# Graph attention on one Trainium2 core: Q by edge made two batches ahead and kept in SBUF, E in two PSUM banks a batch ahead

## The chip, the core and the metric

The kernel runs on one core of a Trainium2 chip. The metric is device time in microseconds (us), from one launch. The engines are named as the profile names them: PE is TensorE (PEld its weight loads), DVE is VectorE, ACT is ScalarE, POOL is GpSimd, SP is SyncE. PSUM has eight banks, and all eight are in use before and after.

## What is computed

The reference is one layer of graph attention with a residual and a layer norm, over 6250 nodes and 206250 edges (sorted by `dst`), 128 features, 8 heads of 16:

```python
Qh, Kh, Vh = h @ WQ, h @ WK, h @ WV            # N x 8 x 16
Eh = edge_attr @ WE                            # E x 8 x 16
score = einsum('ehd,ehd,ehd->eh', Kh[src], Qh[dst], Eh) / sqrt(16)
score = exp(clip(score, -5, 5))
wV = segment_sum(Vh[src] * score[:, :, None], dst, N)
Z  = segment_sum(score, dst, N)
out = layernorm(x + wV / (Z + 1e-6))
```

## The kernel before

The edges are cut into 1612 tiles of 128 edges, and the tiles into 406 batches, of four tiles each but for the last few. At the start a table of K and V rows is made for all nodes (`table`) and written to HBM as `kv`. Each tile then gathers its 128 rows of `kv` by `src` with one indirect DMA that POOL issues (`gather`, L315), four for a batch. The first `XB` = 12 batches gather rows of `x` and make K and V on the core (`project`); the others gather from `kv`.

Q by edge is not gathered. `dst` is sorted, so an edge tile needs few neighbouring nodes. `q_rows` makes Q for a block of 128 nodes, as three bf16 parts, and stores it to HBM (`qs`). `load_q` loads a window of 42 nodes for each 8 tiles, and a matmul of this window with a one-hot of the edges' nodes (`onehotT`) spreads Q over the 512 edges of a batch, with features on partitions. E for the same edges is a matmul of `we_sb` with the edge attributes. Both lie as features x edges.

One round of the main loop serves several batches. In round b the steps below are issued, in this order:

- `turn`(b-1): four transposes bring Q x E of the batch before to edges x features (tile `pps`).
- `stage_a`(b): Q's matmul (tile `qps`), ScalarE's copy of it to SBUF (`qT`), and E's matmul (tile `eps`).
- `finish`, once in some 16 rounds: block sums of two windows of nodes (tile `finps`), then the layer norm's steps, which `fill` strews between VectorE's other work.
- `stage_b`(b-2) on VectorE: `kq` = gathered K rows x `pps`, the sum per head, and the clip (`sc`).
- `messages`(b-3) on VectorE: V rows x weights (`msg`).
- `stage_0`(b+2) on VectorE: the two one-hots (`onehot`, `onehotT`) of a batch two rounds ahead (`AHEAD` = 2).
- `pairs`(b) on VectorE: `eq` = `qT` x `eps`.
- `weigh`(b-2) on ScalarE: the exponentials, twice.
- `stage_c`(b-3): four matmuls add the messages into the window's sum (tile `agg`), and ScalarE copies a finished sum.
- `q_rows`, once in some 8 rounds: Q of the next 128 nodes (tile `qrows`).

From round `XB` on, instructions stand on each engine in the order in which the code issues them (`manual_schedule`); before that a scheduler may move them. Each engine works its list in order. Waits come from tiles: a tile's buffer is used again only when its last reader is done.

PSUM's eight banks are `psE` (1: `eps`), `psQ` (1: `qps`), `psP` (2: `pps`), `psT` (1: `qrows`, `finps`, the transposes of `project`, the count), `psA` (2: `agg`) and `psX` (1: constants and exponentials). The table's blocks and the products of `project` (`kvps`) go in turn through the banks of `psE`, `psP` and `psQ` (`pair_bank`).

Gathers are paced. The pool of gathered rows has `GB` = 15 buffers, so the gather of batch b waits for `messages`(b-15). From batch `LOCK` = 16 on, the first of a batch's four gathers waits also for Q's matmul of batch b - lag(b), where lag falls by one each 4 batches from 12 to `STEP` = 1:

```python
def lag(b):
    return max(STEP, 12 - (b - LOCK) // 4)
...
if i == 0 and b >= LOCK:
    made = expanded[b - lag(b)]
```

SyncE issues the other loads and stores: edge attributes in 512 KB chunks, the nodes of edges spread over partitions (`relb`), Q's windows, rows of `x`, and the output.

Of the kernel before, what the change touches and what calls it, by code (L numbers as in the profile page):

```python
# [24 lines left out]
MW = D + H  # L25
B = 4
CH = 8
GB = 15
XB = 12
LOCK = XB + 4  # L30
STEP = 1
TAIL = 8
HEAD = 132
NG = (NT + G - 1) // G
AHEAD = 2
EB = 6
SLAG = 2
WT = 8
RC = 16
# [41 lines left out]
def edge_attention(ctx: ExitStack, tc: tile.TileContext, x, xT, srcT, dstT, dstB, dst0, bnd, lo, eaT,  # L81
# [30 lines left out]
    with ExitStack() as fast:  # L112
# [78 lines left out]
        def count_inside():  # L191

            W = 4 * 2 * D
            for a in range(0, NT, W):
                e = min(NT, a + W)
                cl = wp.tile([P, W], F32, name="cl", tag="kvst", bufs=2)[:, :e - a]
                count(P, cl, rel[:, a:e], P - 1)
            nc.vector.tensor_reduce(cn[:, :1], cn, axis=AX.X, op=ALU.add)
            pc = psT.tile([1, 1], F32, name="pc", tag="oT")
            nc.tensor.matmul(pc, cn[:, :1], ones, start=True, stop=True)  # L200
            nc.vector.tensor_copy(cnt_i, pc)

# [1 line left out]
        ep = fast.enter_context(tc.tile_pool(name="edges", bufs=EB))  # L204
        wp = fast.enter_context(tc.tile_pool(name="work", bufs=3))
        sp = fast.enter_context(tc.tile_pool(name="sums", bufs=7))
        psE = fast.enter_context(tc.tile_pool(name="psE", bufs=1, space=bass.MemoryType.PSUM))
        psQ = fast.enter_context(tc.tile_pool(name="psQ", bufs=1, space=bass.MemoryType.PSUM))
        psP = fast.enter_context(tc.tile_pool(name="psP", bufs=2, space=bass.MemoryType.PSUM))
        psT = fast.enter_context(tc.tile_pool(name="psT", bufs=1, space=bass.MemoryType.PSUM))  # L210
        psA = fast.enter_context(tc.tile_pool(name="psA", bufs=2, space=bass.MemoryType.PSUM))
        psX = fast.enter_context(tc.tile_pool(name="psX", bufs=1, space=bass.MemoryType.PSUM))

# [3 lines left out]

        def pair_bank(i, name, shape):

            pool, tag = ((psE, "eps"), (psP, "pps"), (psQ, "qps"), (psP, "pps"))[i % 4]  # L220
            return pool.tile(shape, F32, name=name, tag=tag)


# [31 lines left out]

        def q_rows(q):
            n = min(P, N - q * P)
            ps = psT.tile([P, D], F32, name="qrows", tag="oT")
            nc.tensor.matmul(ps[:n], xT_sb[:, LEFT + q * P:LEFT + q * P + n], wq_sb, start=True, stop=True)
            st = wp.tile([P, QP, D], BF16, name="qst", bufs=1)  # L260
            r1 = wp.tile([P, D], F32, name="qr1", bufs=1)
            nc.scalar.copy(st[:n, 0, :], ps[:n])  # L262
            nc.vector.tensor_tensor(r1[:n], ps[:n], st[:n, 0, :], op=ALU.subtract)  # L263
            nc.scalar.copy(st[:n, 1, :], r1[:n])
            nc.vector.tensor_tensor(st[:n, 2, :], r1[:n], st[:n, 1, :], op=ALU.subtract)
            nc.sync.dma_start(qs[q * P * QP:(q * P + n) * QP].rearrange("(p s) f -> p s f", s=QP), st[:n])
            built.append(q)
# [20 lines left out]
        chunks, aggs, sums, pair_sums, st8, expanded = {}, {}, {}, {}, {}, {}  # L288

        def load_chunk(c):  # L290
            if c in chunks or c * CH >= NT:
# [33 lines left out]

        def project(g, n):

            pt = psT.tile([P, B, P], F32, name="xtps", tag="oT")
            for i in range(n):
                nc.tensor.transpose(pt[:, i, :], g[:, i, :D], ident)  # L330
            xgT = wp.tile([P, B, P], F32, name="xgT", tag="kq", bufs=2)
            nc.scalar.copy(xgT[:, :n], pt[:, :n])
            for i in range(0, n, 2):
                k = min(2, n - i)
                pk = pair_bank(i // 2, "kvps", [P, 2, 2 * D])
                for j in range(k):
                    nc.tensor.matmul(pk[:, j, :], xgT[:, i + j, :], wkv_sb, start=True, stop=True)  # L337
                nc.scalar.copy(g[:, i:i + k, :], pk[:, :k, :])  # L338

        def stage_0(b):  # L340
            t0, n = batches[b][0], len(batches[b])
            oh = wp.tile([P, B, P], F32, name="onehot", bufs=AHEAD + 5)
            nc.vector.tensor_tensor(oh[:, :n], iota_p[:, None, :].to_broadcast([P, n, P]),  # L343
                                    rel[:, t0:t0 + n, None].to_broadcast([P, n, P]), op=ALU.is_equal)
            ohT = wp.tile([QROWS, B * P], BF16, name="onehotT", bufs=AHEAD + 2)
            e0 = t0 % RC * P
            nc.vector.tensor_scalar(ohT[:, :n * P], rels[t0 // RC][:, e0:e0 + n * P], node[:QROWS], None,  # L347
                                    op0=ALU.is_equal)
            st8[b] = oh, ohT

        def stage_a(b, g):
            t0, n = batches[b][0], len(batches[b])
            if b < XB:
                project(g, n)
            oh, ohT = st8.pop(b)
            pq = psQ.tile([P, B * P], F32, name="qps")
            expanded[b] = nc.tensor.matmul(pq[:, :n * P], loaded[t0 // WT], ohT[:, :n * P], start=True, stop=True)  # L357
            qT = wp.tile([P, B * P], F32, name="qT", bufs=2)
            nc.scalar.copy(qT[:, :n * P], pq[:, :n * P])  # L359
            pe = psE.tile([P, B * P], F32, name="eps")  # L360
            nc.tensor.matmul(pe[:, :n * P], we_sb, ea_tiles(t0, n), start=True, stop=True)  # L361
            st8[b] = [n, g, oh, pe, qT]

        def pairs(b):

            n, g, oh, pe, qT = st8[b]
            eq = wp.tile([P, B * P], F32, name="eq", bufs=2)
            nc.vector.tensor_tensor(eq[:, :n * P], qT[:, :n * P], pe[:, :n * P], op=ALU.mult)  # L368
            st8[b] = [n, g, oh, eq]
# [37 lines left out]
        def finish(j):  # L407

            q = 2 * j
            ps = psT.tile([P, 2, MW], F32, name="finps", tag="oT")  # L410
            for r in range(3):
                nc.tensor.matmul(ps, shift[:, P - OFF[r]:2 * P - OFF[r]], pair_sums[j][:, r], start=r == 0, stop=False)  # L412
            rest = [(i, (q + i + d, r), d * P + OFF[r]) for i in range(2) for d, r in ((-1, 2), (1, 0))]
            rest = [x for x in rest if x[1] in sums]
            for n, (i, k, s) in enumerate(rest):
                nc.tensor.matmul(ps[:, i], shift[:, P - s:2 * P - s], sums[k], start=False, stop=n == len(rest) - 1)
            fin = sp.tile([P, 2, MW], F32, name="fin", bufs=2)
            nc.scalar.copy(fin, ps)
            pending.append(layernorm(nc, sp, fin, xbs.pop(q), out, q, 2, stores))
# [55 lines left out]
        def fill():  # L475

            if norms and next(norms[0], None) is None:
                norms.pop(0)

        held = []  # L480
        for b in range(nbat + 4):
            if b >= XB and not manual:
# [5 lines left out]
            if b < nbat:  # L488
                load_chunk(batches[b][0] // CH + EB - 3)
                load_rel(batches[b][0] // RC + 1)  # L490
                load_q(batches[b][0] // WT + QLOOK)
                g = gathered.pop(b) if b in gathered else gather(b)
                if b == min(XB, nbat - 1):
                    late_loads()
                if b == min(XB + 8, nbat - 1):
                    relative(C0, NT)
                if b == 14:
                    from_window(1)
                if b == 0:
                    for i in range(AHEAD):  # L500
                        stage_0(i)
                if b > 0:
                    turn(b - 1)
                stage_a(b, g)
            elif b == nbat:
                turn(b - 1)
            norms.extend(pending)
            pending.clear()
            for j in ready:
# [4 lines left out]
            if 0 <= b - 3 < nbat:  # L514
                messages(b - 3)
            fill()
            if b + AHEAD < nbat:
                stage_0(b + AHEAD)
            if b < nbat:
                pairs(b)  # L520
            if 0 <= b - 2 < nbat:
                weigh(b - 2)
            if 0 <= b - 3 < nbat:
                stage_c(b - 3)
            fill()
            if b < nbat:
                while len(built) < q_built(min(NJ - 1, batches[b][0] // WT + QLOOK + 2)):
                    q_rows(len(built))
# [162 lines left out]
```

## Time and profile before

| | before |
|---|---|
| median of 4 runs | 2432.56 us (2426.71 to 2435.3) |
| profiled execution | 2428.43 us, span 2426.6 us |
| PE busy | 1539.1 us (63%) |
| DVE busy | 1556.7 us (64%) |
| ACT busy | 451.8 us (19%) |
| POOL busy | 1531.2 us (63%) |
| mean granted TensorE clock | 0.819 |
| DMA | 398.12 MB, 164 GB/s over the span |

The span goes from the first instruction to the last; the profiled execution's time is 1.8 us longer. A row of the profile gives the line, the engine, the operation, the tiles (out<-in), the shapes and the count; then the busy time in us and the mean of one in ns; then the engine's idle time just before such instructions and what ended most of it. "issue" is time in which the engine waited for nothing that the profile shows, and "remote" or "another core or an unknown queue" is a wait whose end the profile could not put down to an instruction of this core. Ends of matmuls are modelled in the profile, not measured.

### The profile page before, as it was taken

The numbers are of one execution on the slowest core, as the hardware profiler recorded it, in microseconds if no ns is written. First come the engines' busy times: TensorE is split into PE (matmuls) and PEld (weight loads), VectorE is DVE, ScalarE is ACT, GpSimd is POOL, SyncE is SP. The second block draws the span as 40 slices with busy tenths as digits, with TensorE's granted clock in tenths as the row PEclk, the third lists the DMA queues.
The fourth block names the chain that finished last, engine by engine and source line by source line (L and its number), as shares of the span: only waits on it lengthen the run. The fifth ranks groups of instructions, "written<-read, shape, count | busy, mean of one in ns | idle before, by whom it ended". The sixth has DMA issues, their size and how long they took to land.

```text
span 2426.6 us, 24333 instructions
## 1 busy us (share of the span) xinstructions
PE 1539.1 (63%) x6736; PEld 1067.9 (44%) x6736; DVE 1556.7 (64%) x3542; ACT 451.8 (19%) x1548; POOL 1531.2 (63%) x1619
## 2 busy tenths in 40 slices
PE   5587766666656666566666666666666666656665
PEld 3355444444434444344444444444444444444444
DVE  2377777666666666666666656666666666666666
ACT  1232221111111111111111111111111111111111
POOL 6456565666666666666666666666666666666664
PEclk7798888878788888888878888888888878887787
DMA  6656565555555554556556555554655565545542
GB/s 215 178 162 180 163 188 157 147 168 176 158 168 163 180 156 147 172 156 180 150 158 192 160 155 166 176 160 147 186 168 158 149 183 168 167 147 167 174 149 69
DMA packets 177711, 398.12 MB, mean 164 GB/s; under 512 B 60988, under 2 KB 86758, under 8 KB 177568
## 3 DMA queue, kind: packets, MB, share of 16 engines
q0 software_dynamic: 76592, 208.18, 29.9%
q1 hardware_dynamic: 99836, 187.38, 25.1%
q8 instruction: 56, 0.92, 0.2%
q10 hardware_dynamic: 1140, 0.93, 0.1%
q14 instruction: 87, 0.71, 0.1%
HBM read 381.54 MB, written 14.81 MB: 163 GB/s over the span
## 4 chain that ended last, share of the span: by engine, by line
PE 29%; another core or an unknown queue 25%; DVE 24%; issue 15%; ACT 4%; POOL 1%; DMA 1%; DVEq 0%; SPq 0%; ACTq 0%; POOLq 0%
PE eps L361 9%; PE agg L441 7%; PE pps L376 6%; DVE sc L385 5%; DVE kq L382 4%; DVE eq L368 4%; DVE msg L423 3%; PE qps L357 3%; DVE onehot L343 3%; ACT qT L359 2%; DVE onehotT L347 1%; DVE sc L388 1%; PE kvacc L232 1%; PE finps L412 1%
## 5 line engine op out<-in xcount | busy, mean ns | idle before, releaser
L315 POOL DMA_INDIRECT kvrows<-kv,src x1564 | 1484.3, 949 | 848.7 <-issue 405.4
L441 PEld LDWEIGHTS agg<-msg,onehot 128*128 128x128 f32 x3224 | 504.2, 225 | 567.8 <-issue 439.9
L441 PE MATMUL agg<-msg,onehot 128*128 128x136 f32 x3224 | 544.8, 320 | 239.2 <-DVE msg L423 124.8
L376 PE MATMUL pps<-shift,eq 128*128 128x128 f32 x1612 | 325.0, 335 | 572.0 <-DVE eq L368 362.7
L368 DVE TENSOR_TENSOR eq<-qT,eps 128x512 f32<-128x512 f32 x406 | 275.8, 679 | 609.8 <-ACT qT L359 274.2
L361 PE MATMUL eps<-ea,we_sb 128*128 128x512 f32 (+1 forms) x812 | 534.4, 746 | 13.6 <-ACT kvrows L338 10.3
L376 PEld LDWEIGHTS pps<-shift,eq 128*128 128x128 f32 x1612 | 220.0, 169 | 636.7 <-DVE eq L368 394.9
L359 ACT COPY qT<-qps 128x512 f32<-128x512 f32 x406 | 236.8, 583 | 1218.4 <-remote 591.0
L385 DVE TENSOR_REDUCE sc<-kq 128x32 f32<-128x512 f32 x406 | 275.9, 680 | 9.0
L423 DVE TENSOR_TENSOR msg<-kvrows,bank 128x512 f32<-128x512 f32 x406 | 273.9, 675 | 9.1 <-ACT bank L394 8.2
L382 DVE TENSOR_TENSOR kq<-kvrows,pps 128x512 f32<-128x512 f32 x406 | 273.6, 674 | 7.3 <-PE kvps L337 3.3
L343 DVE TENSOR_TENSOR onehot<-bank,dst_sb 128x512 f32<-128x512 f32 x406 | 274.4, 676 | 0.0
L361 PEld LDWEIGHTS eps<-ea,we_sb 128*128 128x128 f32 x812 | 194.3, 241 | 48.3 <-ACT kvrows L338 12.7
L357 PE MATMUL qps<-onehotT,qw 126*128 126x512 bf16 x406 | 189.5, 467 | 1.0 <-ACT qT L359 0.9
L347 DVE TENSOR_SCALAR onehotT<-relb,node 126x512 bf16<-126x512 bf16 x406 | 142.5, 352 | 18.4 <-remote 11.3
L394 ACT ACTIVATE bank<-sc 128x32 f32<-128x32 f32 x406 | 83.0, 204 | 232.8 <-DVE onehot L343 100.4
L396 ACT ACTIVATE msg<-sc 128x32 f32<-128x32 f32 x406 | 87.8, 216 | 0.1
L388 DVE TENSOR_SCALAR sc<-sc 128x32 f32<-128x32 f32 x406 | 77.9, 192 | 9.0
L454 ACT COPY sum<-agg 128x136 f32<-128x136 f32 x146 | 39.0, 267 | 226.3 <-remote 95.2
L315 POOL DMA_INDIRECT kvrows<-x,src x48 | 46.0, 958 | 30.4 <-issue 13.9
L232 PE MATMUL kvacc<-wkv_sb,xT_sb 128*128 128x256 f32 (+1 forms) x98 | 37.1, 536 | 28.3 <-issue 14.8
L263 DVE TENSOR_TENSOR qr<-qrows,qst 128x128 f32<-128x128 f32 (+1 forms) x49 | 14.1, 288 | 61.2 <-ACT qst L262 36.9
(69 smaller groups left out, 531.1 us busy)
## 6 DMA issues: line engine op xcount, KB each, us to landing
ea<-eaT SPq DMA_DIRECT2D x201, 512.0 KB
relb<-relD SPq DMA_DIRECT2D x100, 504.0 KB
kvrows<-kv,src POOLq DMA_INDIRECT x1564
qw<-qs SPq DMA_DIRECT2D x202, 31.5 KB
kv<-kvst SPq DMA_DIRECT2D x12, 512.0 KB
qs<-qst SPq DMA_DIRECT2D x48, 96.0 KB
xb<-x SPq DMA_DIRECT2D x24, 128.0 KB
out<-h SPq DMA_DIRECT2D x24, 128.0 KB
```

The costliest lines, as they stand in the source:

```text
L315: ins = nc.gpsimd.indirect_dma_start(out=g[:k, i, :f], out_offset=None, in_=rows, in_offset=bass.IndirectOffsetOnAxis(ap=src_col(t)[:k], a ...
L343: nc.vector.tensor_tensor(oh[:, :n], iota_p[:, None, :].to_broadcast([P, n, P]), rel[:, t0:t0 + n, None].to_broadcast([P, n, P]), op=ALU.i ...
L347: nc.vector.tensor_scalar(ohT[:, :n * P], rels[t0 // RC][:, e0:e0 + n * P], node[:QROWS], None, op0=ALU.is_equal)
L357: expanded[b] = nc.tensor.matmul(pq[:, :n * P], loaded[t0 // WT], ohT[:, :n * P], start=True, stop=True)
L359: nc.scalar.copy(qT[:, :n * P], pq[:, :n * P])
L361: nc.tensor.matmul(pe[:, :n * P], we_sb, ea_tiles(t0, n), start=True, stop=True)
L368: nc.vector.tensor_tensor(eq[:, :n * P], qT[:, :n * P], pe[:, :n * P], op=ALU.mult)
L376: nc.tensor.transpose(pp[:, i, :], eq[:, i * P:i * P + P], ident)
L382: nc.vector.tensor_tensor(t1[:, :n], g[:, :n, :D], pp[:, :n], op=ALU.mult)
L385: nc.vector.tensor_reduce(sc[:, :n], t1[:, :n].rearrange("p b (h d) -> p b h d", h=H), axis=AX.X, op=ALU.add)
L423: nc.vector.tensor_tensor(m[:, :n, :D].rearrange("p b (h d) -> p b h d", h=H), g[:, :n, D:].rearrange("p b (h d) -> p b h d", h=H), exp_p[ ...
L441: nc.tensor.matmul(aggs[k], oh[:, i, :], m[:, i, :], start=first and not final, stop=last)
```

## The change

Q and E are no longer made in the round that uses them. `stage_a` is split. `expand_q`(b+2) makes Q by edge two batches ahead (`QA` = 2), at the end of the round, and its copy `qT` has four buffers instead of two. `expand_e`(b+1) makes E one batch ahead (`EA` = 1), right behind `turn`(b-1), and `psE` has two banks instead of one. The second bank comes from `psT`, which is gone: the block sums of `finish`, Q's rows of `q_rows`, the transposes of `project` and the count now use the bank of `psQ`. `pair_bank` takes `psE` and `psP` in turn.

`stage_0` is split too. `one_hot_rows`(b+2) still makes `onehotT` two batches ahead, with three buffers instead of four; `one_hot`(b) makes `onehot` in the batch's own round, just ahead of `pairs`(b), with six buffers instead of seven. `eq` has three buffers instead of two. `GB` is 14 instead of 15. `expanded`, for which the gathers wait, now holds E's matmul instead of Q's, and `STEP` is 0 instead of 1. Before the loop, `onehotT` and Q of batches 0 and 1 and E of batch 0 are made.

```diff
-GB = 15
+GB = 14
-STEP = 1
+STEP = 0
-AHEAD = 2
+QA = 2
+EA = 1
...
-        psE = fast.enter_context(tc.tile_pool(name="psE", bufs=1, space=bass.MemoryType.PSUM))
+        psE = fast.enter_context(tc.tile_pool(name="psE", bufs=2, space=bass.MemoryType.PSUM))
...
-        psT = fast.enter_context(tc.tile_pool(name="psT", bufs=1, space=bass.MemoryType.PSUM))
...
-            pool, tag = ((psE, "eps"), (psP, "pps"), (psQ, "qps"), (psP, "pps"))[i % 4]
+            pool, tag = ((psE, "eps"), (psP, "pps"))[i % 2]
...
         def q_rows(q):
-            ps = psT.tile([P, D], F32, name="qrows", tag="oT")
+            ps = psQ.tile([P, D], F32, name="qrows", tag="qps")
...
-        def stage_0(b):
+        def one_hot(b):
             t0, n = batches[b][0], len(batches[b])
-            oh = wp.tile([P, B, P], F32, name="onehot", bufs=AHEAD + 5)
+            hot[b] = wp.tile([P, B, P], F32, name="onehot", bufs=6)
...
+        def one_hot_rows(b):
+            t0, n = batches[b][0], len(batches[b])
+            hotT[b] = wp.tile([QROWS, B * P], BF16, name="onehotT", bufs=3)
...
-        def stage_a(b, g):
+        def expand_q(b):
             t0, n = batches[b][0], len(batches[b])
-            if b < XB:
-                project(g, n)
-            oh, ohT = st8.pop(b)
             pq = psQ.tile([P, B * P], F32, name="qps")
-            expanded[b] = nc.tensor.matmul(pq[:, :n * P], loaded[t0 // WT], ohT[:, :n * P], start=True, stop=True)
-            qT = wp.tile([P, B * P], F32, name="qT", bufs=2)
-            nc.scalar.copy(qT[:, :n * P], pq[:, :n * P])
-            pe = psE.tile([P, B * P], F32, name="eps")
-            nc.tensor.matmul(pe[:, :n * P], we_sb, ea_tiles(t0, n), start=True, stop=True)
+            nc.tensor.matmul(pq[:, :n * P], loaded[t0 // WT], hotT.pop(b)[:, :n * P], start=True, stop=True)
+            qTs[b] = wp.tile([P, B * P], F32, name="qT", bufs=QA + 2)
+            nc.scalar.copy(qTs[b][:, :n * P], pq[:, :n * P])
+
+        def expand_e(b):
+            t0, n = batches[b][0], len(batches[b])
+            pes[b] = psE.tile([P, B * P], F32, name="eps")
+            expanded[b] = nc.tensor.matmul(pes[b][:, :n * P], we_sb, ea_tiles(t0, n), start=True, stop=True)
...
-            ps = psT.tile([P, 2, MW], F32, name="finps", tag="oT")
+            ps = psQ.tile([P, 2, MW], F32, name="finps", tag="qps")
...
+        for b in range(QA):
+            one_hot_rows(b)
+            expand_q(b)
+        for b in range(EA):
+            expand_e(b)
...
-                if b > 0:
-                    turn(b - 1)
-                stage_a(b, g)
-            elif b == nbat:
+            if 0 < b <= nbat:
                 turn(b - 1)
+            if b < nbat and b < XB:
+                project(g, len(batches[b]))
+            if b + EA < nbat:
+                expand_e(b + EA)
...
-            if b + AHEAD < nbat:
-                stage_0(b + AHEAD)
+            if b + QA < nbat:
+                one_hot_rows(b + QA)
             if b < nbat:
-                pairs(b)
+                one_hot(b)
+                pairs(b, g)
...
             fill()
+            if b + QA < nbat:
+                expand_q(b + QA)
             if b < nbat:
                 while len(built) < q_built(min(NJ - 1, batches[b][0] // WT + QLOOK + 2)):
                     q_rows(len(built))
```

More of the change, by code (lines that the diff above doesn't have):

```diff
@@ L198, in count_inside @@
             nc.vector.tensor_reduce(cn[:, :1], cn, axis=AX.X, op=ALU.add)
-            pc = psT.tile([1, 1], F32, name="pc", tag="oT")
+            pc = psQ.tile([1, 1], F32, name="pc", tag="qps")
             nc.tensor.matmul(pc, cn[:, :1], ones, start=True, stop=True)
@@ L286, in load_rel @@
                               .to_broadcast([QROWS, n]))
-        chunks, aggs, sums, pair_sums, st8, expanded = {}, {}, {}, {}, {}, {}
+        chunks, aggs, sums, pair_sums, hotT, hot, qTs, pes, st8, expanded = ({} for _ in range(10))
         def load_chunk(c):
@@ L326, in project @@
         def project(g, n):
-            pt = psT.tile([P, B, P], F32, name="xtps", tag="oT")
+            pt = psQ.tile([P, B, P], F32, name="xtps", tag="qps")
             for i in range(n):
@@ L338, in project @@
                 nc.scalar.copy(g[:, i:i + k, :], pk[:, :k, :])
-        def stage_0(b):
+        def one_hot(b):
             t0, n = batches[b][0], len(batches[b])
-            oh = wp.tile([P, B, P], F32, name="onehot", bufs=AHEAD + 5)
-            nc.vector.tensor_tensor(oh[:, :n], iota_p[:, None, :].to_broadcast([P, n, P]),
+            hot[b] = wp.tile([P, B, P], F32, name="onehot", bufs=6)
+            nc.vector.tensor_tensor(hot[b][:, :n], iota_p[:, None, :].to_broadcast([P, n, P]),
                                     rel[:, t0:t0 + n, None].to_broadcast([P, n, P]), op=ALU.is_equal)
-            ohT = wp.tile([QROWS, B * P], BF16, name="onehotT", bufs=AHEAD + 2)
+        def one_hot_rows(b):
+            t0, n = batches[b][0], len(batches[b])
+            hotT[b] = wp.tile([QROWS, B * P], BF16, name="onehotT", bufs=3)
@@ L346, in stage_0 @@
             e0 = t0 % RC * P
-            nc.vector.tensor_scalar(ohT[:, :n * P], rels[t0 // RC][:, e0:e0 + n * P], node[:QROWS], None,
+            nc.vector.tensor_scalar(hotT[b][:, :n * P], rels[t0 // RC][:, e0:e0 + n * P], node[:QROWS], None,
                                     op0=ALU.is_equal)
-            st8[b] = oh, ohT
-        def stage_a(b, g):
+        def expand_q(b):
             t0, n = batches[b][0], len(batches[b])
-            if b < XB:
-                project(g, n)
-            oh, ohT = st8.pop(b)
@@ L356, in stage_a @@
             pq = psQ.tile([P, B * P], F32, name="qps")
-            expanded[b] = nc.tensor.matmul(pq[:, :n * P], loaded[t0 // WT], ohT[:, :n * P], start=True, stop=True)
-            qT = wp.tile([P, B * P], F32, name="qT", bufs=2)
-            nc.scalar.copy(qT[:, :n * P], pq[:, :n * P])
-            pe = psE.tile([P, B * P], F32, name="eps")
[L361 to L369, printed above, removed]
+            nc.tensor.matmul(pq[:, :n * P], loaded[t0 // WT], hotT.pop(b)[:, :n * P], start=True, stop=True)
@@ new lines, in expand_q, with pairs @@
+            qTs[b] = wp.tile([P, B * P], F32, name="qT", bufs=QA + 2)
[4 more added lines that the diff above has]
+            expanded[b] = nc.tensor.matmul(pes[b][:, :n * P], we_sb, ea_tiles(t0, n), start=True, stop=True)
+        def pairs(b, g):
+            n = len(batches[b])
+            eq = wp.tile([P, B * P], F32, name="eq", bufs=3)
+            nc.vector.tensor_tensor(eq[:, :n * P], qTs.pop(b)[:, :n * P], pes.pop(b)[:, :n * P], op=ALU.mult)
+            st8[b] = [n, g, hot.pop(b), eq]
@@ L498, in edge_attention @@
                     from_window(1)
-                if b == 0:
-                    for i in range(AHEAD):
-                        stage_0(i)
-                if b > 0:
-                    turn(b - 1)
-                stage_a(b, g)
-            elif b == nbat:
+            if 0 < b <= nbat:
                 turn(b - 1)
+            if b < nbat and b < XB:
+                project(g, len(batches[b]))
+            if b + EA < nbat:
+                expand_e(b + EA)
             norms.extend(pending)
```

## The prediction

> **What bounds the kernel now.** I read the page first, then the wait list, then the timeline of some rounds, then every gather's row. The page's totals come first (share of the chain that ended last; then busy time, mean ns, and idle time with its releaser).
>
> ```profile
> PE 29%; another core or an unknown queue 25%; DVE 24%; issue 15%; ACT 4%; POOL 1%; DMA 1%; DVEq 0%; SPq 0%; ACTq 0%; POOLq 0%
> L315 POOL DMA_INDIRECT kvrows<-kv,src x1564 | 1484.3, 949 | 848.7 <-issue 405.4
> L368 DVE TENSOR_TENSOR eq<-qT,eps 128x512 f32<-128x512 f32 x406 | 275.8, 679 | 609.8 <-ACT qT L359 274.2
> L359 ACT COPY qT<-qps 128x512 f32<-128x512 f32 x406 | 236.8, 583 | 1218.4 <-remote 591.0
> L382 DVE TENSOR_TENSOR kq<-kvrows,pps 128x512 f32<-128x512 f32 x406 | 273.6, 674 | 7.3 <-PE kvps L337 3.3
> ```
>
> No engine is full (DVE 64%, PE 63%, POOL 63%), and a quarter of the chain has no name. VectorE never waits for gathered rows (L382: 7.3 us in all); it waits at `eq` for Q's copy, and ScalarE waits there for "remote". The timeline shows what that is (start, length, engine, [idle before, releaser]):
>
> ```profile
> 1208.72 0.38 PE L357 MATMUL qps<-onehotT,qw 126*128 126x512 bf16 x1
> ...
> 1212.61 0.95 POOL L315 DMA_INDIRECT kvrows<-kv,src  x1 [0.30 <-issue]
> 1215.99 0.59 ACT L359 COPY qT<-qps 128x512 f32<-128x512 f32 x1 [9.32 <-remote]
> 1216.22 0.95 POOL L315 DMA_INDIRECT kvrows<-kv,src  x1 [2.67 <-remote]
> ...
> 1216.61 0.69 DVE L368 TENSOR_TENSOR eq<-qT,eps 128x512 f32<-128x512 f32 x1 [5.44 <-ACT qT L359]
> ```
>
> Q's matmul ends at 1209.10, yet the copy that waits for it alone starts at 1215.99: TensorE's signal came 6.9 us late, 2.4 us after POOL's last gather ended (1213.56). POOL waited for a TensorE signal too and went on 0.23 us later. The same at the start of the kernel, where 16 gathers run without a pause:
>
> ```profile
> 87.27 0.94 POOL L315 DMA_INDIRECT kvrows<-kv,src  x1 [9.34 <-DMA ea<-eaT]
> ...
> 106.02 0.95 POOL L315 DMA_INDIRECT kvrows<-kv,src  x1 [0.30 <-issue]
> 112.19 0.94 POOL L315 DMA_INDIRECT kvrows<-kv,src  x1 [5.22 <-issue]
> ```
>
> ```profile
> 99.34 2.96 PE L337 MATMUL kvps<-wkv_sb,xgT 128*128 128x256 f32 x8
> 111.89 1.22 PE L361 MATMUL eps<-ea,we_sb 128*128 128x512 f32 x1 [9.59 <-ACT kvrows L338]
> ```
>
> ScalarE starts again at 110.04, 22.77 us after the first of 16 gathers: 1.42 us a gather, though POOL issues one each 1.25 us. I cut all L315 rows into runs (a gap over 0.8 us ends a run) and compared each Q matmul's end with its copy's start. After 330 us there are 20 runs of 4, 37 of 8 and 86 of 12 gathers, with mean periods (start to start) of 6.81, 11.58 and 17.49 us. Of 406 Q signals 175 came over 1 us late, 600 us in all. In runs of 12, those up to 5.2 us after the run's start were prompt, those of 5.6 to 8.5 came by 10.1, those of 9.2 to 16.7 at 17.1 to 18.0. So TensorE's signals pass only when POOL's work has been worked off, and POOL pauses only because each gather batch waits for a TensorE signal. I do not know why; I use it as a measured rule. The bound is then POOL's train of gathers with its pauses, 1.45 to 1.70 us a gather; the rest waits inside it.
>
> **The change, part by part.** *Slack against a late signal.* Rounds that run free take 3.60 us (`kq` at 1199.82, the next at 1203.42). Before, `eq` starts 3.0 us into its round; Q (0.66 `turn` + 0.38), its copy (0.59) and E must all arrive within that round: some 1.1 to 1.4 us of slack. After, `eq`(b) reads a Q copied rounds ago and an E made a round ago; the tightest signal is `turn`(b-1), done 0.7 us into round b and wanted by `kq` at 3.6: 2.9 us. Holds of 3 to 8 us are not covered whole, but VectorE gets most of a round further in each, and TensorE has one or two more E's done when a hold ends. POOL then gets two batches at once more often: fewer runs of 4.
>
> What that is worth is set by POOL. The 1408 gathers of those runs took 136.2 + 428.5 + 1504.0 = 2068.7 us. In long runs alone, (428.5 + 1504.0)/1328 = 1.455 us each, they would take 2049: -20. At the shortest period of 12 (17.33, 1.444) they take 2034: -35. With nothing gained, 0. I take -28, since the change should also trim pauses that a late matmul prolongs.
>
> *Head.* From 87 to 330 us pauses exceed what such runs need (1.85, 2.0, 2.7, 3.3 us after 4, 8, 12, 16) by about 20 us, and there VectorE's pace decides, as POOL runs up to 12 batches ahead. Between 0 and -20 I take -10.
>
> *Permission.* A late gather batch waited for Q(b-1), now for E(b) (`STEP` 0): the same place in TensorE's round b-1, after `turn`(b-2), but E needs 0.86 to 1.71 us where Q needs 0.22 to 0.43. Where a release ends the pause this costs nothing. The 22 waits of POOL put down to Q alone (53.7 us) can each grow by about 1 us: 0 to +22, taken +4, because Q matmuls ended 0.4 to 8 us before most releases.
>
> *Q's bank shared.* `finish` (24 times) and `q_rows` (45 in the loop) now use Q's bank. `q_rows` stands behind `expand_q`(b+2) in TensorE's order, so TensorE waits for its own signal: Q, ScalarE's copy, then `qrows`; `turn`(b) and E are queued behind, and VectorE's `qr` behind those. Prompt, that is 0.65 us x 45 = 29 us, under the 2 us that VectorE has spare a round (5.88 - 3.83). Held signals are the price: 175 of 406 late by 3.4 us on average make 19 of 45 and 10 of 24, 29 x 3.4 = 99 us if nothing hides them. Most of it falls where TensorE and VectorE would stand anyway: 0 to +99, taken +8.
>
> *The rest.* The one-hots keep their counts (406 x 676 and 352 ns); Q(b+2) now needs `onehotT` of the same round, 2.4 us in, while TensorE is in `agg` until 3.3 or later: nothing, or 0.3 us a round of TensorE's spare time. In the first 12 rounds `kvps` takes a bank of E's pair, so E(b+1) waits for `eq`(b); 0.86 to 1.71 us x 12 is +10 to +20 if bare, but those rounds last 7 us and more and Q leaves that path: -5 to +20, taken +3. `GB` 14 lets gather b start after `messages`(b-14), which binds only where the lag is 11 or 12 (to batch 23): one round, +5, or -5, as a shorter first run releases the signals before 110 us; taken 0. Deeper buffers for qT and eq add no instruction.
>
> Sum: -28 - 10 + 4 + 8 + 3 = -23 on the profiled execution's 2428.4 us (span 2426.6) = 2405. The median of the runs shown, 2432.6, is 4 higher: 2409.
>
> **Two rules against rows.** Two windows bear on whether a denser VectorE slows POOL (VectorE busy 7.15 of 8.70 us, then 3.60 of 8.50):
>
> ```profile
> 1198.80:1207.50 8.70, 6.31 (x33) 4.00 (x32) 7.15 (x15) 2.66 (x10) 6.64 (x7) 0.98 0.35 94
> 1207.50:1216.00 8.50, 3.12 (x17) 2.09 (x17) 3.60 (x7) 0.01 (x1) 4.73 (x5) 1.00 0.33 94
> ```
>
> In both, gathers follow each other after 0.30 us, so I add nothing. The Trainium skill, "SBUF — State Buffer", section on the two sides of SBUF, speaks against the change: VectorE in a two-port mode locks GpSimd out and starves its descriptors. By that, one `onehotT` in the way each batch would be an estimated 0.35 x 406 = 143 us, which no row here shows and which the change would not alter in number.
>
> The second is the 1.42 us a gather, which I keep as a floor. The skill's "DMA: Bandwidth & Descriptors", in its anatomy of one DMA, fits 2.0 us fixed and bytes/436e3 beyond; by estimate 131 KB then cost 0.3 us, and nothing would hold trains of gathers to 1.42.
>
> **Rivals.** (a) *Held by its own bank* (slower, 0.31). Place: TensorE at `qrows` and `finps`, waiting for a copy whose signal is held. Price: up to 99 us. It decides once more than a third of that, 31 us, is uncovered, as the other terms give -31. For it: ScalarE already waits 37.0 us at `qst` and 54.5 at `fin` for "remote". Against: 2 us spare a round. With two thirds uncovered, 66 - 31 = +35: 2468.
> (b) *Nothing moves* (0.13). The mix of runs stays, as POOL's own train sets it; VectorE only waits elsewhere, at `kq`. For it: runs of 8 and 12 differ by 0.01 us a gather. Time 2432 within 7.
> (c) *The holds vanish* (0.04). POOL would run at its issue rate, 1408 x (1.469 - 1.253) = 304 us less: 2128. Against: the 16 gathers that took 1.42 each while VectorE and TensorE stood still.
>
> **Numbers.** The forecast has 0.52, own range 2372 to 2425 (its terms at their favourable ends, -35 - 20 - 5, to just under no change). About 0.3%, 7 us, is what a measurement here can tell from no change. Faster 0.52 + 0.04 = 0.56, same 0.13, slower 0.31. The range 2365 to 2468 leaves out (c) and the worse part of (a), together 0.17.
>
> **What would show it.** Right: ScalarE's wait at `qT` for "remote" falls well below 591 us but costs nothing on VectorE; VectorE's idle time before `eq` drops below 200 us, some of it turning up at `kq`; runs of 4 gathers become rarer and some of 16 appear; a period per gather stays at 1.44 to 1.46 us in long runs. Wrong: TensorE idle before `qrows`, `finps` or Q by 50 us or more with more short runs (rival a); the same mix of runs (b); long runs under 1.40 us a gather (c).

## The result, and the profile after

The changed kernel takes 2440.2 us (median of 42 runs, 2425.7 to 2454.1), the kernel before 2430.6 us (63 runs). The ratio is 1.0038, with a 95% interval of 1.0029 to 1.0047: slower by about 9 us. The profiled execution took 2439.2 us, its span 2437.4 us. The forecast of 2409 had the wrong direction; its range (2365 to 2468) holds the time.

The page of the changed kernel, in the lines that answer to those shown of before (L385 is `kq`, L371 `eq`):

```profile
DVE 27%; PE 23%; issue 21%; another core or an unknown queue 17%; ACT 4%; DMA 4%; POOL 2%; SPq 1%; DVEq 0%; ACTq 0%; POOLq 0%
L315 POOL DMA_INDIRECT kvrows<-kv,src x1564 | 1487.1, 951 | 857.6 <-issue 380.7
L385 DVE TENSOR_TENSOR kq<-kvrows,pps 128x512 f32<-128x512 f32 x406 | 274.5, 676 | 422.8 <-remote 228.4
L371 DVE TENSOR_TENSOR eq<-qT,eps 128x512 f32<-128x512 f32 x406 | 271.6, 669 | 9.2 <-PE qps L357 4.9
L357 PE MATMUL qps<-onehotT,qw 126*128 126x512 bf16 x406 | 184.2, 454 | 415.9 <-ACT qT L359 231.8
L359 ACT COPY qT<-qps 128x512 f32<-128x512 f32 x406 | 237.0, 584 | 923.6 <-remote 639.7
```

The wait at `eq` is gone, as forecast: 609.8 us before, 9.2 now. But it has moved. `kq` now waits 422.8 us (7.3 before), and TensorE waits 415.9 us ahead of Q's matmul (1.0 before), 231.8 us of them put down to ScalarE's copy of the Q before, which frees Q's bank. POOL's idle time is as long as it was (848.7 before, 857.6 now). Q's matmul stands in the page of before so:

```profile
L357 PE MATMUL qps<-onehotT,qw 126*128 126x512 bf16 x406 | 189.5, 467 | 1.0 <-ACT qT L359 0.9
```

Signals of Q over 1 us late fell from 175 to 124, but they add up to 714 us instead of 600. They also come later for the same place. Of the Q matmuls that end 7.0 to 8.9 us into a run of 12 gathers (after 330 us), the late ones all had their copy started by 10.15 us before (7 of 10 late). In the changed kernel 53 of 59 are late, half of them come after 15.7 us, and only three by 10.15. Why is not known.

I cut POOL's rows into runs of gathers as in the prediction. After 330 us there are 16 runs of 4, 43 of 8, 82 of 12 and one of 16 (before 20, 37, 86 and none). The same 1408 gathers take 2078.8 us, before 2068.7: 1.476 us a gather against 1.469. Those 10 us answer to the loss; the spans differ by 10.8. The mix of runs hardly moved. What grew are pauses. A run of 12 needs 12 x 1.4275 = 17.13 us to be worked off (in the trace of before, copies of Q that were held to the end of such a run start 17.09 to 18.04 us into it), and POOL goes on about 0.25 us later; one of 8 goes by the same sum, and one of 4 needs 6.5 us in all. Pauses that exceed this need by over 0.5 us were 3 before, 7.4 us in all, and are 11 after, 23.1 us in all; a twelfth, behind a run of two, is in the last batches. Six of the 11 (14.2 us) stand behind runs of 12, where before had none. Without these excesses the train would take 2055.7 us after and 2061.3 before, so some 6 us were gained elsewhere in it. One trace of each kernel can't divide 10 us exactly, as the runs behind the medians spread over 19 us before and 28 us after. This is one of the six, from the timeline (start, length, engine, [idle before, releaser]); its run of 12 began at 1429.63:

```profile
1443.40 0.95 POOL L315 DMA_INDIRECT kvrows<-kv,src  x1 [0.30 <-issue]
1446.90 0.39 ACT L421 COPY fin<-finps 128x272 f32<-128x272 f32 x1 [13.05 <-remote]
...
1447.34 0.59 PE L357 MATMUL qps<-onehotT,qw 126*128 126x512 bf16 x1 [7.74 <-ACT fin L421]
...
1447.72 1.06 PE L379 MATMUL pps<-shift,eq 128*128 128x128 f32 x4
...
1448.57 1.85 PE L365 MATMUL eps<-ea,we_sb 128*128 128x512 f32 x2
...
1450.70 1.14 POOL L315 DMA_INDIRECT kvrows<-kv,src  x1 [6.36 <-DVE eq L371]
```

The signal that `finps` is done was held until 1446.90. Only then could ScalarE free Q's bank; then came Q, `turn`, and E, which ended at 1450.42, and E is what POOL waits for now. POOL went on 3.8 us after the release. (The profile names `eq` as POOL's releaser, since it ended 0.01 us earlier; the wait that the code makes is on E.) Five of the six pauses have `finps` in this place, one has `qrows`, and in all six POOL goes on 0.27 or 0.28 us after E's end. In one of them (its run began at 1724.95) the signal came 14.3 us into the run, before the run's last gather had ended, so a release doesn't always wait for the whole run.

### The profile page after: what moved, and what is told of

Its sections match the earlier page's. It is cut to its first block, busy times and chain, and to the rows that moved or that the text cites. A ratio compares the mean times of both kernels' runs of the same rounds, so it can differ in the third digit from the quotient of the medians.

```text
span 2437.4 us, 24091 instructions
## 1 busy us (share of the span) xinstructions
PE 1537.8 (63%) x6736; PEld 1024.5 (42%) x6736; DVE 1565.5 (64%) x3542; ACT 460.8 (19%) x1548; POOL 1533.6 (63%) x1619
## 4 chain that ended last, share of the span: by engine, by line
DVE 27%; PE 23%; issue 21%; another core or an unknown queue 17%; ACT 4%; DMA 4%; POOL 2%; SPq 1%; DVEq 0%; ACTq 0%; POOLq 0%
PE agg L444 7%; PE eps L365 6%; DVE sc L388 5%; DVE kq L385 5%; DVE onehot L343 4%; PE pps L379 4%; DVE eq L371 3%; DVE msg L426 3%; DMA kvrows<-kv,src 3%; PE qps L357 3%; POOL kvrows L315 2%; ACT qT L359 2%; DVE onehotT L350 2%; PE kvps L337 1%
## 5 line engine op out<-in xcount | busy, mean ns | idle before, releaser
L315 POOL DMA_INDIRECT kvrows<-kv,src x1564 | 1487.1, 951 | 857.6 <-issue 380.7
L444 PEld LDWEIGHTS agg<-msg,onehot 128*128 128x128 f32 x3224 | 495.3, 223 | 618.3 <-issue 502.9
L385 DVE TENSOR_TENSOR kq<-kvrows,pps 128x512 f32<-128x512 f32 x406 | 274.5, 676 | 422.8 <-remote 228.4
L365 PE MATMUL eps<-ea,we_sb 128*128 128x512 f32 (+1 forms) x812 | 523.1, 733 | 0.0
L357 PE MATMUL qps<-onehotT,qw 126*128 126x512 bf16 x406 | 184.2, 454 | 415.9 <-ACT qT L359 231.8
L379 PEld LDWEIGHTS pps<-shift,eq 128*128 128x128 f32 x1612 | 241.3, 170 | 462.6 <-issue 411.1
L359 ACT COPY qT<-qps 128x512 f32<-128x512 f32 x406 | 237.0, 584 | 923.6 <-remote 639.7
L379 PE MATMUL pps<-shift,eq 128*128 128x128 f32 x1612 | 313.6, 328 | 10.7 <-issue 2.8
L371 DVE TENSOR_TENSOR eq<-qT,eps 128x512 f32<-128x512 f32 x406 | 271.6, 669 | 9.2 <-PE qps L357 4.9
L350 DVE TENSOR_SCALAR onehotT<-relb,node 126x512 bf16<-126x512 bf16 x406 | 162.1, 400 | 7.4 <-PE qps L357 3.8
L365 PEld LDWEIGHTS eps<-ea,we_sb 128*128 128x128 f32 x812 | 156.0, 237 | 1.1
L263 DVE TENSOR_TENSOR qr<-qrows,qst 128x128 f32<-128x128 f32 (+1 forms) x49 | 14.3, 291 | 213.8 <-ACT qst L262 168.8
L259 PEld LDWEIGHTS qrows<-wq_sb,xT_sb 128*128 128x128 f32 (+1 forms) x98 | 20.2, 253 | 174.0 <-ACT qT L359 125.4
L259 PE MATMUL qrows<-wq_sb,xT_sb 128*128 128x128 f32 (+1 forms) x98 | 31.5, 415 | 78.7 <-issue 39.6
L415 PE MATMUL finps<-sum,shift 128*128 128x272 f32 x144 | 52.4, 516 | 34.7 <-ACT qT L359 26.6
```

The source lines that it names most:

```text
L315: ins = nc.gpsimd.indirect_dma_start(out=g[:k, i, :f], out_offset=None, in_=rows, in_offset=bass.IndirectOffsetOnAxis(ap=src_col(t)[:k], a ...
L350: nc.vector.tensor_scalar(hotT[b][:, :n * P], rels[t0 // RC][:, e0:e0 + n * P], node[:QROWS], None, op0=ALU.is_equal)
L357: nc.tensor.matmul(pq[:, :n * P], loaded[t0 // WT], hotT.pop(b)[:, :n * P], start=True, stop=True)
L359: nc.scalar.copy(qTs[b][:, :n * P], pq[:, :n * P])
L365: expanded[b] = nc.tensor.matmul(pes[b][:, :n * P], we_sb, ea_tiles(t0, n), start=True, stop=True)
L371: nc.vector.tensor_tensor(eq[:, :n * P], qTs.pop(b)[:, :n * P], pes.pop(b)[:, :n * P], op=ALU.mult)
```

## The experiments

All ratios are to the kernel before on the same chip; the times are medians. The comparisons ran on several chips, and these are of two kinds: on some the kernel before takes 2407 to 2431 us and TensorE's signals are held, on the others it takes 2044 to 2047 us and they are not. Each run is told with its kind, and only runs on the same kind of chip are set against each other.

| run | what it is | us, before | ratio (95%) |
|---|---|---|---|
| *signals held* | | | |
| first comparison | the changed kernel | 2440.2, 2430.6 | 1.0038 (1.0029 to 1.0047) |
| `b_gb14` | before, 14 buffers | 2403.2, 2407.5 | 0.9986 (0.9968 to 1.0003) |
| `q_gb15` | Q alone ahead, permission by E | 2419.3, 2407.5 | 1.0059 (1.0039 to 1.0080) |
| `q_pace_2` | Q alone ahead, permission by Q | 2434.2, 2429.1 | 1.0016 (1.0002 to 1.0031) |
| *not held* | | | |
| `after_again` | the changed kernel | 2053.1, 2043.6 | 1.0042 (1.0028 to 1.0055) |
| `a_step1` | changed, `STEP` 1 | 2050.3, 2044.2 | 1.0030 (1.0020 to 1.0040) |
| `q_bank` | Q ahead, bank shared, permission by E | 2055.6, 2045.1 | 1.0050 (1.0036 to 1.0064) |
| `q_only` | the same, bank not shared | 2048.7, 2044.2 | 1.0020 (1.0011 to 1.0028) |
| `q_pace` | the same, 15 buffers, permission by Q | 2046.4, 2044.5 | 1.0008 (0.9998 to 1.0017) |
| `a_permQ`, `a_permQ_2` | changed, permission by Q | 2049.5, 2045.1; 2052.9, 2046.8 | 1.0020 (1.0011 to 1.0029); 1.0029 (1.0019 to 1.0039) |
| `b_permE`, `b_permE_2` | before, permission by E | 2046.8, 2045.1; 2049.8, 2046.8 | 1.0003 (0.9994 to 1.0012); 1.0013 (1.0004 to 1.0022) |
| `b_bank` | before, bank shared | 2062.6, 2044.2 | 1.0086 (1.0073 to 1.0099) |
| `a_qa1` | changed, Q one ahead | 2050.8, 2044.2 | 1.0026 (1.0017 to 1.0035) |
| `three_of_four` | changed, a gather fewer per batch | 1774.8, 2043.6 | 0.8696 (0.8674 to 0.8718) |
| `bf16_rows` | changed, half the gathered bytes | 2050.0, 2043.6 | 1.0029 (1.0019 to 1.0040) |

`before_again` is one more profiled run of the kernel before (2401.8 us). It was expected to show a chip without holds and fell on a chip that has them, as did `b_gb14` and `q_gb15`, whose expectations name times without holds. The other way round, `q_only`, `b_bank`, `a_step1`, `a_qa1`, `b_permE_2` and `a_permQ_2` were to decide between causes with holds and met a chip without them, so what they were to settle there stays open.

### Without holds: the same kernels, the same loss

`before_third` and `after_again` are the two kernels unchanged.

> The kernel before, for its trace on the chip of this comparison. Without holds: POOL's train with fewer than 3 us of pauses, last gather's end near 2027. With holds: runs of 4, 8 and 12 gathers, 1.45 to 1.47 us a gather.

> The changed kernel itself, on the chip of this comparison. In the first four comparisons the kernel before took 2044 us, not 2431, POOL's gathers ran without pauses at 1.253 us each and no signal of TensorE was held. If the loss of 9 us needs the held signals, the changed kernel is within 3 us of before on such a chip; if it comes from instructions and waits that are there without holds, it is 4 to 8 us slower there too (variants of it were 4.5 to 6.6 us slower). On a chip that holds the signals: 9 us slower, as before.

The kernel before, then the changed one, both without holds:

```profile
L315 POOL DMA_INDIRECT kvrows<-kv,src x1564 | 1485.9, 950 | 479.5 <-issue 367.7
L382 DVE TENSOR_TENSOR kq<-kvrows,pps 128x512 f32<-128x512 f32 x406 | 275.9, 680 | 351.2 <-DMA kvrows<-kv,src 347.5
L359 ACT COPY qT<-qps 128x512 f32<-128x512 f32 x406 | 236.7, 583 | 537.4 <-PE qps L357 535.9
```

```profile
L315 POOL DMA_INDIRECT kvrows<-kv,src x1564 | 1487.4, 951 | 483.1 <-issue 356.6
L385 DVE TENSOR_TENSOR kq<-kvrows,pps 128x512 f32<-128x512 f32 x406 | 275.7, 679 | 317.9 <-DMA kvrows<-kv,src 292.6
```

No wait ends by "remote". POOL gathers on without a break at 1.253 us each; behind its 100th gather the kernel before has no pause over 0.8 us at all. VectorE waits for the rows themselves. So POOL's issue is the bound, and what is made ahead of it gains nothing here. The last gather ends at 2029.3, where the held run of before has it at 2410.9: with holds the train takes 382 us more, 76 of them in the first 200 gathers.

The loss is 9 us here too. It is in the train's first 400 gathers (506.4 us before, 510.2 after) and behind its last (14.8 us to the end before, 16.7 after; 15.7 and 16.8 with holds). Gathers 400 to 1611 take 1518.3 and 1519.7 us. In the changed kernel POOL stops where the pace reaches its last steps, batches 63 and 64 (lag 1, then 0), where the kernel before has no pause:

```profile
326.69 0.94 POOL L315 DMA_INDIRECT kvrows<-kv,src  x1 [2.23 <-DVE onehotT L350]
...
333.38 0.95 POOL L315 DMA_INDIRECT kvrows<-kv,src  x1 [1.91 <-PE eps L365]
```

These two profiled spans, taken on two chips, differ by 7.2 us; the medians on one chip differ by 9.4. The change also lowered the mean granted TensorE clock, to 0.874 from 0.886 without holds and to 0.801 from 0.819 in the profiled runs with them. `q_pace` below has a lower clock too (0.877 against 0.885) and is not measurably slower, so a clock lower by that much does not make the loss by itself; no run tests it alone.

### The change, taken apart part by part

```diff
 b_bank:  before, with qrows and finps in psQ's bank (tag "qps")
 b_permE: before, expanded[b] = nc.tensor.matmul(pe, ...)     # E's, not Q's
 b_gb14:  before, GB = 14
 q_only:  after, EA = 0, STEP = 1, psE 1 bank, psT back for qrows, finps, xtps, pc
 q_bank:  q_only, with qrows and finps in psQ's bank
 q_gb15:  q_only, GB = 15, qT 3 buffers, eq 2
 q_pace:  q_gb15, expanded[b] = Q's matmul, lag = max(0, 11 - (b - LOCK) // 4)
 a_step1: after, STEP = 1
 a_permQ: after, expanded[b] = Q's matmul
 a_qa1:   after, QA = 1
```

> The changed kernel with Q still two batches ahead in SBUF, but E made in its own round in one bank, the second bank given back to `qrows`, `finps`, the transposes of `project` and the count, and `STEP` = 1. The prediction's slack theory: Q ahead without the shared bank and without the later permission should keep the gain, 2431 - 20 = 2410. Theory of the gather train (POOL's 1.42 us a gather sets the time, and what is made ahead gains nothing): within 5 us of before, 2431. Theory 3 (Q made ahead itself costs it): 2440.

> The run with Q alone ahead, with 15 buffers of gathered rows again (room from two buffers of `eq` in place of three and three of `qT` in place of four). If the buffer count is what this variant still loses (4.5 us), it comes to 2044 within 2; if not, it stays at 2049.

> Q two batches ahead and the one-hots as in the changed kernel, but 15 buffers of gathered rows, a bank of its own for `qrows` and `finps`, E in its own round, and permission of the gathers by Q's matmul at the place in the rounds that it has in the kernel before. If the permission by E was what the runs with Q alone ahead lost: within 3 us of before, on any chip. If Q's place costs it: 4 us slower without holds (about 2049), 10 to 14 us slower with them. The prediction's slack theory: 10 to 28 us faster where signals are held.

> Q two batches ahead at the pace of the kernel before, again. With signals held: within 3 us of before if the permission by E's matmul made the loss of the runs with Q alone ahead, 10 to 14 us slower if Q's place makes it, 10 to 28 us faster by the prediction's slack theory. Without holds: 1.9 us slower, as in the run before, within 2 us.

Q two batches ahead by itself brings nothing on either kind of chip. Without holds `q_pace` is within the uncertainty of before. With holds, where the expectation by the slack theory was 10 to 28 us faster, it is slower by 0.5 to 7.5 us. It has only Q's half of the slack, since E is still made in its own round. The waits moved (`q_pace_2`, with holds; L372 is `eq`, L358 Q's matmul):

```profile
L372 DVE TENSOR_TENSOR eq<-qT,eps 128x512 f32<-128x512 f32 x406 | 275.7, 679 | 577.4 <-remote 401.5
L358 PE MATMUL qps<-onehotT,qw 126*128 126x512 bf16 x406 | 177.9, 438 | 201.2 <-ACT qT L360 106.6
```

`eq` waits 577 us (609.8 before), now mostly for "remote" instead of Q's copy. Q's copy is made rounds ahead, which leaves E's signal as the likely late one. `q_gb15` differs from `q_pace` in the permission alone. With holds that is 1.0059 against 1.0016, some 10 us (4 to 17, the two intervals combined), though measured on two chips.

Where the time goes is not the same in these kernels. The traces tell how much later a gather starts than in the kernel before (`q_gb15` against `before_again`, on one chip; the others against the first profile of before). Gather 300 stands past the last step of the pace, gather 1608 is among the last.

| later than before, us | gather 300 | gather 1608 | last gather |
|---|---|---|---|
| changed kernel | -4.4 | 7.3 | 9.6 |
| `q_gb15` | 11.2 | 14.4 | 16.7 |
| `q_pace_2` | 13.8 | 15.3 | 15.6 |

With Q alone ahead most is lost before gather 300, and from gather 300 to 1608 the train runs within 1.5 to 3.2 us of before, whichever matmul gives the permission. The changed kernel is ahead at gather 300 and loses 11.7 us behind it, where its six long pauses are. So the permission by E does not make that loss alone. Something that `q_gb15` lacks (the shared bank, E ahead, fewer buffers) has to be with it; the pauses point to the bank, but no run with holds separates them. That is one trace of each kernel; that of `q_pace_2` is the slowest of its 12 runs, and its chip is another than that of the first profile.

> The kernel before, with the permission of the gathers tied to E's matmul instead of Q's: the prediction priced this at +4 (0 to +22) where signals are held. If it is the permission that cost the 9 us, 4 to 10 us slower than before; if not, within 2 us. On a chip without holds POOL never waits for it after the first batches: within 2 us.

> Permission of the gathers by E's matmul in the kernel before, again, for a chip that holds the signals. There, if the permission makes the loss: 5 to 12 us slower than before (about 1.003 to 1.005), with more pauses of POOL over 0.5 us beyond what the work-off needs. If Q's place two batches ahead makes it: within 3 us. On a chip without holds: 1.7 us slower, as in the run before.

> The changed kernel with the permission of the gathers tied to Q's matmul of batch b-lag instead of E's (`STEP` still 0), which stands about 1 to 2 us earlier in TensorE's order. If the later permission by E makes POOL's extra pauses (12 of them, 26 us, against 3 of 7 us before, in the first comparison), the time falls by 4 to 9 us, to that of before. If the pauses come from TensorE's own waits for Q's bank, it stays within 3 us of the changed kernel, about 1.004 times before.

> The changed kernel with permission by Q's matmul, again, for a chip that holds the signals. There, if the permission makes the loss: back to before, within 3 us. If Q's place makes it: 7 to 12 us slower than before, as the changed kernel and the run with Q alone ahead. On a chip without holds: 4.4 us slower, as in the run before.

All four ran on chips without holds. There the medians put the permission by E alone at 1.7 and 2.9 us (the first is not clear of zero), and undoing it in the changed kernel brings it from 9.4 to 4.4 and 6.1 us (only the first of these two falls is clear of noise). It does not bring all back: with `STEP` 0 POOL still stops at batch 64, for 4.97 and 4.96 us in the two profiled runs. On a chip that holds signals neither the permission alone, nor the shared bank alone, nor the changed kernel with the permission undone was run.

> The changed kernel, with `STEP` = 1 in place of 0, so that a late gather batch waits for E's matmul of the batch before, a round earlier. Theory 2 (the later permission costs the 9 us): back to before, 2431 or lower, and fewer pauses of POOL over 0.5 us. Theory 1 (shared bank) and theory 3 (work ahead): stays at 2440 within 4. If TensorE's held signals grow with longer runs of gathers, an earlier permission gives longer runs (16 and more) and the time could rise instead, by 5 to 20 us.

> The run with Q alone ahead (`q_only`: 4.5 us slower than before without holds), with `qrows` and `finps` in Q's bank as in the changed kernel. If the shared bank costs, 3 to 14 us more than that: 1.004 to 1.009 times before. If it is Q's place two batches ahead that costs, the same 1.002 to 1.006 as without the sharing.

> The kernel before, with one edit: Q's rows (`qrows`) and the block sums (`finps`) use the bank of `psQ`, as in the changed kernel. Theory 1 (the shared bank is what the change lost): 6 to 14 us slower than before, about 2440, with TensorE idle before `qrows`, `finps` and Q longer by tens of us. Theory 2 (the permission by E's matmul is what it lost) and theory 3 (making Q and E ahead lost it): within 4 us of before, 2431. Rival (a) of the prediction at full size would be +66 or more.

`b_bank` is 18 us slower, more than any theory had. Its first `kq` starts at 80.7 us instead of 63.2, and 16.1 us remain at the last batch: all of it is there before the first `kq`, and nothing is lost in 400 rounds. The changed kernel has no such late start (64.2). `q_bank` against `q_only` puts the shared bank at 6 us in the new order. From `q_only` (4.5 us slower) the rest adds up: the shared bank +6.0, E ahead in two banks, with the transposes of `project` and the count moved to Q's bank, -4.4 (`a_step1`, 6.1), `STEP` 0 +3.3 (`after_again`, 9.4). Each of these steps is uncertain by about 3.5 us, so only the bank's and E's stand clear of zero, and several were measured on different chips.

> The changed kernel with Q one batch ahead instead of two (`QA` = 1). Slack theory: less slack against a held signal, 5 to 15 us slower than the changed kernel (2445 to 2455). Gather-train theory: the depth of what is made ahead is worth nothing, within 4 us of the changed kernel (2440), while VectorE's idle time moves back from `kq` to `eq`.

> The kernel before with 14 buffers of gathered rows in place of 15. If the buffer that was given up makes the pauses of POOL (gather b then waits for the messages of b-14), 2 to 6 us slower than before, about 2048, with pauses near 145 and 325 us. If the later permission and the shared bank make them, within 2 us of before.

Neither shows a cost. Without holds `a_qa1` is 6.6 us slower than before where the changed kernel is 9.4, and the two intervals overlap; with holds Q's depth was not varied. The 14 buffers, run with holds, cost the kernel before nothing.

### What would move the time

> The changed kernel, with the fourth gather of each batch from batch 16 on replaced by a plain load of 128 neighbouring rows of `kv` that SyncE issues: the bytes and the work of the other engines stay, about 390 of POOL's gathers go (its fourth tile holds rows of other nodes). Gather-train theory, with signals held: 390 x 1.42 = 554 us less, about 1885; without holds 390 x 1.253 = 489 us less, which would go under what VectorE needs (1558 us busy and some 90 us ahead of the loop), so 1650 to 1750. If VectorE or TensorE set the time, within 30 us of the changed kernel.

> The changed kernel, with the table of K and V and the gathered rows in bf16, so that each gather moves half the bytes (K and V are rounded to bf16). If the train of gathers is paced by their count (issue and descriptors), the time stays within 10 us of the changed kernel. If it is paced by bytes, the work-off of 1.42 us a gather falls to the issue rate of 1.253 or less: up to 235 us faster on a chip that holds the signals, and nothing on one that doesn't, except for VectorE's waits for gathered rows (300 to 340 us in all) growing shorter.

```diff
 three_of_four: in gather(b), for b >= LOCK and i == 3
+    nc.sync.dma_start(g[:, i, :f], rows[b * 15:b * 15 + P, :f]); continue
 bf16_rows: kv, its staging tile and kvrows (from batch XB on) in BF16
```

Two lines of `three_of_four`, then one of `bf16_rows`:

```profile
PE 1336.3 (75%) x6736; PEld 863.7 (49%) x6736; DVE 1544.6 (87%) x3542; ACT 464.7 (26%) x1548; POOL 1168.6 (66%) x1234
L318 POOL DMA_INDIRECT kvrows<-kv,src x1179 | 1121.7, 951 | 568.6 <-issue 246.3
```

```profile
L315 POOL DMA_INDIRECT kvrows<-kv,src x1564 | 1485.1, 950 | 482.7 <-issue 345.6
```

`three_of_four` leaves out the gather by `src` of each batch's fourth tile from batch 16 on; the tile holds rows of other nodes instead, so the result is not that of the layer. With 385 gathers fewer it is 278 us faster than the changed kernel, at the same bytes (398 MB). At 1774.8 us it misses the 1650 to 1750 that were expected; VectorE is then the busiest engine, at 87%, and likely the next bound. Half the gathered bytes move neither the gathers (950 ns each) nor the time. The count of gathers sets it, not what they carry. Both ran without holds, so whether the 1.42 us of a held gather depends on its bytes stays open.

## Why the prediction was wrong, step by step

*The bound* was named rightly: POOL's train of gathers. `three_of_four` shows it without holds; with holds the trace's loss lies in the train as well.

*Steady state, -28: the step that failed.* I took VectorE's and TensorE's slack to be what starts the next gathers. It isn't. POOL's permission is a TensorE signal, so it passes when POOL's work has been worked off, however far VectorE has got meanwhile; I had that rule from the trace, and still let the slack shorten the runs. For that I had no row. The pauses that a late matmul prolongs, which the term was to trim, grew (7.4 to 23.1 us). Runs of 4 went from 20 to 16, but those of 12 from 86 to 82, and 1.469 us a gather became 1.476. Of the signs I had named, the wait at `eq` went as for a gain, but ScalarE's wait for "remote" at `qT` rose to 639.7 us instead of falling, and only one run of 16 appeared. The whole slack, Q's and E's, was run only in the changed kernel: what its train gained beside the longer pauses is some 6 us in the one pair of traces, where the term had -28. Q's half by itself, with holds, is `q_pace_2`: between +0.5 and +7.5 us. From gather 300 on the sum's steady terms, -28 + 4 + 8 = -16, came out at +11.7.

*Head, -10.* With holds near 0: `kq` of batch 60 starts at 416.3 us in both, though gather 300 starts 4.4 us earlier. Without holds some 4 to 6 us worse.

*Permission, +4 (0 to +22).* In the range as far as it was run: 1.7 and 2.9 us without holds in the kernel before, some 10 with them for Q alone ahead, of which the steady part has little. I had priced one late matmul a wait; the six long pauses show the whole chain of Q, `turn` and E behind a bank that comes free at the release.

*Q's bank, +8 (0 to +99).* Sign and size right without holds, 6 us. With holds it was not run alone; the six pauses, 14.2 us, stand behind the bank and the permission together. Of rival (a)'s signs TensorE's idle time ahead of Q came (416 us), but no more short runs. More than half of that idle time is put down to the copy of the Q before it in its one bank, and `q_pace_2`, which shares nothing, has 106.6 us of that kind too. The sharing shows in the waits of Q behind `fin` and in those of `qrows` behind Q's copy; what of them delays POOL, beyond the six pauses, is not shown:

```profile
PE qps L357 <- ACT qT L359: 231.8, 51, 8.0
PEld qrows L259 <- ACT qT L359: 125.4, 28, 9.4
PE qps L357 <- ACT fin L421: 33.6, 5, 9.2
```

*The small terms.* `GB` 14 taken 0: measured -4 (-8 to +1). First 12 rounds +3: `kq` of batch 12 is 0.6 us later without holds and 2.4 us earlier with them. The tail, 1 to 2 us, I had no term for.

So the two losses, +12 together, were of the right size, with their shares open, and of the two gains, -38, little was there. Rival (b), with 0.13, came nearest: POOL's train stays and VectorE only waits elsewhere, at `kq`. It had left out that the two losses then stand uncovered. Rival (c) put the holds at 304 us in the steady state; on chips without them that part is 306 us (382 less the 76 of the start), but no edit here brings it about.

## What to carry to other kernels

When waits end late because of a shared train of work, ask what the train itself waits for: slack elsewhere moves the wait to another line and leaves the time. A permission that paces a bottleneck engine should hang on the earliest instruction that is late enough, with nothing queued ahead of it that waits for the same kind of signal. And a bank given to two uses puts each behind the other's copy: 6 us in 2045 here when signals were prompt, and long pauses where a signal was late.

## What the runs showed of the hardware

The same kernel took 2044 us on some chips and 2407 to 2431 us on others, each within 0.5% of its median. On the latter, TensorE's signals were held behind POOL's gathers (about 1.43 us for each gather of a full run until release), on the former never in the profiled runs, and gathers followed each other at 1.253 us. I have no explanation of what sets the chips apart: the traffic is the same (398 MB), and so is the time of one gather on POOL (949 and 950 ns). Besides the holds, the mean granted TensorE clock differs, 0.819 against 0.887 for the kernel before; whether that is a cause or a consequence no run shows. A tuning step of 1% that is judged on one chip can rest on a state that the next chip doesn't have; this change's ratio happened to be the same on both, by different pauses.
